# High and low parts of the row maxima by two reductions, in a two-layer cross-attention kernel

## The chip, the core and the metric

The kernel runs on one core of a Trainium2 chip. A core has five engines with instruction streams of their own that meet through semaphores: PE (TensorE: matmuls, with the weight loads listed apart as PEld), DVE (VectorE: element-wise work and reductions along the free dimension), ACT (ScalarE: activations and copies), POOL (GpSimd: element-wise work between SBUF tiles here) and SP (SyncE, which issues nearly all DMAs). Data lies in SBUF, in 128 partitions; matmuls write PSUM, which has eight banks of 128 x 512 fp32. The metric is the device time of one execution in microseconds, as a median of runs.

## The reference

Two layers over x of 4 x 512 x 320, each of them self attention, cross attention to a context of 4 x 1601 x 192, and a gated feed-forward part. There are 20 heads of 16 channels. Of one layer, cut to what matters:

```python
h1 = _ln(x, n1_g, n1_b)
x = _attn(h1, h1, q1, k1, v1, o1_w, o1_b, heads) + x
h2 = _ln(x, n2_g, n2_b)
x = _attn(h2, context, q2, k2, v2, o2_w, o2_b, heads) + x
h3 = _ln(x, n3_g, n3_b)
a, g = jnp.split(h3 @ ff_w1 + ff_b1, 2, axis=-1)
x = a * jax.nn.gelu(g, approximate=False) @ ff_w2 + ff_b2 + x
```

where `_attn` has, for each head, `sim = q k^T * scale`, `a = softmax(sim)` and `out = a v`. The softmax needs each query's maximum over the keys, or something close to it, to be taken off before the exponential; any value near it serves, since it cancels in the quotient.

## The kernel before

**Units.** Attention is cut into 80 units: layer (2) x kind (self, cross) x batch element (4) x group of four heads (5). A feed-forward unit for each layer and batch element follows the attention of its layer. Self attention has 512 keys, or 4 chunks of 128; cross attention 1601, or 13 chunks, the last with 65 rows.

**High and low parts.** Matmuls take fp32 operands in a rounded form, F32R. Queries and keys are split into a rounded high part and a low part that holds what the rounding left, and products of both are added up. POOL does this splitting (lines 803 and 804).

**A unit's two passes over the scores.** In the first pass scores stand with queries on the partitions: PE writes 128 x 512 of them into a bank (`sps`, L1054), and DVE reduces the bank to 128 maxima (L1069). In self units a maximum goes straight into the tile `nmax`, 16 columns for 4 heads x 4 blocks of 128 queries. In cross units the maxima of four stretches of keys go to `pm`, with a shorter one for the rest (L1091), and `max_reduce` (L1109) brings them together into `nmax`. In the second pass scores stand with keys on the partitions (`st`, L1280): two products of keys and queries, and a third of a tile of ones with `nrows`, which takes the maximum of each query off. ACT raises the bank (L1290), and a chunk later PE multiplies the result with the values (`av`, L1306); ACT copies that (L1325), and POOL adds it up (L1326).

**From columns to rows.** `max_end` lies between the passes. A maximum stands in a query's partition and must come to stand in a row, queries along the free dimension, and in two parts, since `nrows` is read as F32R. In `max_end`, L1119 writes the rounded maxima into a tile `parts` (the conversion), L1120 takes them from the maxima and writes the difference beside them (the subtraction), L1123 turns `parts` in blocks of 32 x 32 into `turned`, and four DMAs on SP carry rows of it into `nrows` (L1131). The minus sign comes in earlier: L1069 of a self unit and L1109 of a cross unit write the maxima negated.

**Order.** Everything is issued in one written order. While a unit's second pass runs over its chunks, the first pass of the next one or two units is mixed in, pair by pair of heads (`round_of` sets the matmuls of both in turns). Three chunks from a unit's end, `main` calls `max_reduce` and `max_end` for the next unit, whose first-pass products have all been issued by then; after that come the last two chunks, with first-pass products of the unit after next. Beside the chunks a list of errands is worked off: projections, layer norms, output projections, and POOL's divisions by the softmax's sums (L1191). Banks of PSUM are given out when the program is made, by estimated times of PE, ACT and DVE (`expect`, `busy`, `written`); a matmul into a bank waits until the last reader of it is done.

`nmax` and `nrows` exist twice and are used in turn; `parts` and `turned` come from a pool with two buffers.

Of the kernel before, what the change touches and what calls it, by code (L numbers as in the profile page):

```python
# [9 lines left out]
F32 = mybir.dt.float32  # L10
F32R = mybir.dt.float32r
I32 = mybir.dt.int32
AF = mybir.ActivationFunctionType
ALU = mybir.AluOpType
AX = mybir.AxisListType
# [8 lines left out]
P = 128  # L24
NQ = N // P
G, HG = 5, 4
GD = HG * DH
SLOT = 32
# [47 lines left out]
def kernel(ctx: ExitStack, tc: tile.TileContext, x, context, ws, out):  # L76
# [18 lines left out]
    nc = tc.nc  # L95
    dma = nc.sync.dma_start

    const = ctx.enter_context(tc.tile_pool(name="const", bufs=1))
    wpool = ctx.enter_context(tc.tile_pool(name="weights", bufs=1))
    one = ctx.enter_context(tc.tile_pool(name="one", bufs=1))  # L100
    two = ctx.enter_context(tc.tile_pool(name="two", bufs=2))
# [19 lines left out]
    nc.gpsimd.memset(columns_of, 1.0)  # L121
    vals = columns_of[:, : NC2 * H * VW].rearrange("p (c h w) -> p c h w", h=H, w=VW)

    nmax = [const.tile([P, HG * NQ], F32, name=f"nmax{i}") for i in range(2)]
    nrows = [const.tile([P, N], F32R, name=f"nrows{i}") for i in range(2)]
    for t in nrows:
        nc.gpsimd.memset(t.bitcast(F32), 0.0)
# [271 lines left out]
    def bank(name):  # L399
        i = min(range(NB), key=lambda i: bank_free[i])  # L400
        assert bank_free[i] < HELD, name
        t = psum.tile([P, 512], F32, tag=f"bank{i}", name=name)
        bank_of[id(t)] = [i, t, bank_free[i], 0.0]
        bank_free[i] = HELD
        return t
# [6 lines left out]
    def busy(engine, us, *tiles):  # L412
        expect[engine] = max([expect[engine]] + [bank_of[id(t)][3] + 0.05 for t in tiles]) + us
        for t in tiles:
            bank_free[bank_of[id(t)][0]] = expect[engine] + 0.09
# [624 lines left out]
    def max_pairs(u):  # L1040

        full = u.nkeys // 512
        rest = u.nkeys - full * 512
        ns = full + (1 if rest else 0)
        u.nm = nmax[u.n % 2]
        u.rows = nrows[u.n % 2]
        u.pm = two.tile([P, NQ, HG, ns], F32, tag="pm", name="pm") if ns > 1 else None

        def full_two(heads, t, s):
            pss = []  # L1050

            def product(e):
                for j, ps in zip(heads, pss):
                    nc.tensor.matmul(  # L1054
                        ps,
                        lhsT=u.q[j * SLOT : (j + 1) * SLOT, e, t * P : (t + 1) * P],
                        rhs=u.kT[j * SLOT : (j + 1) * SLOT, u.k0 + s * 512 : u.k0 + (s + 1) * 512],
                        start=(e == 0),
                        stop=(e == 1),
                    )  # L1060

            if ns == 1:
                to = u.nm.rearrange("p (j t) -> p j t", t=NQ)[:, :, t]
            else:
                to = u.pm[:, t, :, s]

            def reduce():
                for j, ps in zip(heads, pss):
                    nc.vector.tensor_reduce(to[:, j : j + 1], ps, AX.X, ALU.max, negate=(ns == 1))  # L1069
                    busy("dve", 0.6, ps)  # L1070

            return heads, [lambda e=e: product(e) for e in range(2)], reduce, pss, lambda: pss.extend(bank("sps") for _ in heads)

        def rest_two(heads):
            pss = []
            w = rest + rest % 2

            def product(t):
                for e in range(2):
                    for j, ps in zip(heads, pss):  # L1080
                        nc.tensor.matmul(  # L1081
                            ps[:, t * w : (t + 1) * w],
                            lhsT=u.q[j * SLOT : (j + 1) * SLOT, e, t * P : (t + 1) * P],
                            rhs=u.kT[j * SLOT : (j + 1) * SLOT, full * 512 : full * 512 + w],
                            start=(e == 0),
                            stop=(e == 1),
                        )

            def reduce():
                for j, ps in zip(heads, pss):  # L1090
                    nc.vector.tensor_reduce(  # L1091
                        u.pm[:, :, j, full], ps[:, : NQ * w].rearrange("p (t w) -> p t w", w=w)[:, :, :rest], AX.X, ALU.max,
                    )
                    busy("dve", 0.38, ps)

            return heads, [lambda t=t: (product(t), product(t + 1)) for t in range(0, NQ, 2)], reduce, pss, lambda: pss.extend(bank("sps") for _ in heads)

        pairs = [
            deque([lambda heads=heads, t=t, s=s: full_two(heads, t, s)] for s in range(full) for t in range(NQ))
            for heads in ((2, 3), (0, 1))  # L1100
        ]
        if rest:
            for q, heads in zip(pairs, ((2, 3), (0, 1))):
                q.append([lambda heads=heads: rest_two(heads)])
        return pairs

    def max_reduce(u):
        if u.pm is not None:
            nc.vector.tensor_reduce(  # L1109
                u.nm.rearrange("p (j t) -> p t j", t=NQ), u.pm, AX.X, ALU.max, negate=True  # L1110
            )
            busy("dve", 0.25)

    def max_end(u):

        parts = two.tile([P, SLOT], F32, tag="parts", name="parts")
        high, low = (parts.rearrange("p (j e t) -> p e j t", e=2, t=NQ)[:, e] for e in range(2))
        of = u.nm.rearrange("p (j t) -> p j t", t=NQ)
        nc.vector.tensor_copy(high.bitcast(F32R), of)  # L1119
        nc.vector.tensor_tensor(low, of, high, ALU.subtract)  # L1120
        turned = two.tile([P, SLOT], F32, tag="turned", name="turned")

        nc.vector.transpose(turned, parts)  # L1123
        busy("dve", 0.6)
        slots = u.rows.bitcast(F32).rearrange("(g s) n -> s g n", s=DH)[0].rearrange("g (t r) -> g t r", t=NQ)

        def rows():
            for i in range(P // SLOT):
                part = slice(i * SLOT, (i + 1) * SLOT)
                queue = (nc.sync, nc.scalar, nc.gpsimd, nc.sync)[i] if start["on"] else nc.sync  # L1130
                queue.dma_start(out=slots[:, :, part], in_=turned[part, :])  # L1131

        if u.cross and u.before.cross:
            errands.appendleft((clock["round"] + 1, yes, rows))
        else:
            rows()
# [133 lines left out]
    def main(u, give, nxt):  # L1270
# [59 lines left out]
        for c in range(u.nch):  # L1330
# [29 lines left out]
            if not last and c == u.nch - 3:  # L1360
                max_reduce(nxt)
                max_end(nxt)
# [52 lines left out]
    def ff_main(u, give, nxt):  # L1415
        done = 0

        def beside(room, n):

            nonlocal done  # L1420
            if room:
                for extra in give(done, True)[1]:
                    round_of(extra)
            done += n
            if done == u.steps - 1 and nxt is not None and nxt.kind != "ff":
                max_reduce(nxt)
                max_end(nxt)
            steps(True)
            for _ in range(n - 1):
                steps(False)  # L1430
# [235 lines left out]
    at_once(units[2])  # L1666
    run("values")
    max_reduce(first)
    max_end(first)
    loads.extend(load_x(2))  # L1670
    for fs in (load_out(0, "o1_w"), load_x(3), load_cross(0)):
# [57 lines left out]
```

## Time and profile before

| | |
|---|---|
| median of 3 runs | 3000.01 us (2998.21 to 3005.65) |
| profiled execution, its own time | 3000.91 us |
| its span, first to last instruction | 2999.1 us |
| granted TensorE clock, mean | 0.993 |
| self attention, layer 0 and layer 1 | about 60 to 375 and 1525 to 1867 us of the span |
| cross attention, layer 0 and layer 1 | about 375 to 1200 and 1867 to 2690 us |
| feed-forward, layer 0 and layer 1 | about 1200 to 1525 and 2690 to 2999 us |

How to read the profile's lines: a group has the kernel's line, the engine, the operation, the tiles written and read (out<-in), shapes as partitions x elements, and the count; behind the bar stand the busy time in us, the mean duration of one in ns, and the engine's idle time ahead of these instructions with what ended it. A row of the view of one line has minimum, median and maximum duration in ns. A row of the timeline has the start and the length in us, counted from the start of the span, and in brackets the idle time ahead of it and who ended it; instructions of one group that follow each other are merged (x8). A row of windows has the stretch, its length, and an engine's busy time with the count. Where an instruction is held up after its engine has taken it, the profile books the delay as part of its duration.

### The profile page before, as it was taken

The page shows a single profiled execution, that of the slowest core. Times are in us where ns is not written, and L with a number is a line of the kernel's source. Part 1 is how long each engine was busy: PE and PEld are TensorE (multiplying, and loading weights), DVE is VectorE, ACT ScalarE, POOL GpSimd, SP SyncE. Part 2 cuts the span into 40 slices and gives each one's busy share as a digit, 9 for nine tenths or more (in the row PEclk, how much of TensorE's full clock was granted, in tenths as well). Part 3 has the DMA queues.
Part 4 walks back from the last instruction along what each step waited for, and adds up shares of the span by engine and source line. Part 5 has one row for each costly group of instructions (what it writes and reads, how often), then busy time and mean ns, then how long its engine had stood idle before and what let it go on. Part 6 is the DMA issues. An engine that isn't in the chain of part 4 may idle for free.

```text
span 2999.1 us, 84363 instructions
## 1 busy us (share of the span) xinstructions
PE 2885.4 (96%) x35018; PEld 1509.7 (50%) x35018; DVE 2150.8 (72%) x4143; ACT 1892.7 (63%) x3746; POOL 1194.0 (40%) x1305
## 2 busy tenths in 40 slices
PE   8999999999999999999999899999999999999999
PEld 4455554555554554355554555555555555544555
DVE  6877888889889888323268788888888888873221
ACT  3766677877877878501147676778778778784000
POOL 3444344544544545211224443445445454451110
PEclk9999999999999999999999999999999999999999
DMA  4444223132232122200123342222221121222000
GB/s 107 103 122 102 71 74 96 46 90 60 53 82 67 39 56 60 82 17 15 37 60 74 91 99 66 66 58 53 53 64 46 49 70 44 54 54 76 22 22 14
DMA packets 186543, 188.70 MB, mean 63 GB/s; under 512 B 69668, under 2 KB 137264, under 8 KB 186160
## 3 DMA queue, kind: packets, MB, share of 16 engines
q1 hardware_dynamic: 185368, 182.11, 24.0%
q8 instruction: 276, 4.52, 0.6%
q10 hardware_dynamic: 760, 1.18, 0.2%
q14 instruction: 107, 0.88, 0.1%
q0 software_dynamic: 32, 0.00, 0.0%
HBM read 55.76 MB, written 29.36 MB: 28 GB/s over the span
## 4 chain that ended last, share of the span: by engine, by line
PE 77%; DVE 18%; DMA 1%; issue 1%; ACT 1%; POOL 1%; SPq 1%; ACTq 0%; DVEq 0%; POOLq 0%
PE av L1306 21%; PE st L1280 15%; PE fps L1391 9%; DVE pm L1069 9%; PE sps L1054 6%; PE yps L1498 6%; PE vps L1015 4%; DVE nmax L1069 4%; PE ops L1209 3%; PE kps L951 3%; PE qkps L886 3%; PE fps L1451 2%; PE qps L927 2%; PE sps L1081 1%; DVE hturned L608 1%
## 5 line engine op out<-in xcount | busy, mean ns | idle before, releaser
L1290 ACT ACTIVATE pr<-st 128x512 f32<-128x512 f32 (+1 forms) x2720 | 1405.0, 603 | 429.1 <-PE st L1280 381.4
L1069 DVE TENSOR_REDUCE pm<-sps 128x1 f32<-128x512 f32 x1920 | 1185.3, 681 | 129.6 <-PE sps L1054 121.5
L1326 POOL TENSOR_TENSOR o<-o,vo 128x512 f32<-128x512 f32 x576 | 740.7, 1286 | 1125.9 <-ACT vo L1325 1114.3
L1054 PE MATMUL sps<-kT,q 32*128 32x512 f32 x4800 | 874.4, 429 | 13.7 <-DMA q<-low 4.3
L1306 PE MATMUL av<-pr,vals 128*32 128x512 f32 (+1 forms) x5440 | 738.4, 609 | 74.7 <-DVE nmax L1069 19.3
L1280 PE MATMUL st<-q,kT 32*128 32x512 f32 (+1 forms) x5120 | 795.7, 421 | 7.1 <-DVE pm L1069 6.4
L1280 PEld LDWEIGHTS st<-q,kT 32*128 32x128 f32 (+1 forms) x5120 | 422.9, 180 | 299.5 <-issue 120.1
L1280 PE MATMUL st<-nrows,ones 32*128 32x512 f32 (+1 forms) x2720 | 542.6, 399 | 5.4 <-DMA nrows<-turned 5.4
L1054 PEld LDWEIGHTS sps<-kT,q 32*128 32x128 f32 x4800 | 424.0, 183 | 102.2 <-DVE pm L1069 26.8
L1069 DVE TENSOR_REDUCE nmax<-sps 128x1 f32<-128x512 f32 x640 | 395.2, 680 | 81.1 <-PE sps L1054 77.9
L1325 ACT COPY vo<-av 128x512 f32<-128x512 f32 x576 | 352.3, 612 | 26.8 <-PE av L1306 24.7
L1462 ACT ACTIVATE gl<-fps,b 128x512 f32<-128x512 f32 x80 | 54.8, 687 | 414.3 <-PE fps L1451 303.0
L1306 PEld LDWEIGHTS av<-pr,vals 128*32 128x32 f32 (+1 forms) x5440 | 111.1, 108 | 348.8 <-DVE pm L1069 180.7
L1391 PE MATMUL fps<-hT,w 128*128 128x512 f32 x640 | 283.2, 597 | 0.0
L1280 PEld LDWEIGHTS st<-nrows,ones 32*128 32x128 f32 (+1 forms) x2720 | 247.0, 180 | 28.2 <-DMA nrows<-turned 4.8
L1463 DVE SCALAR_TENSOR_TENSOR hid<-fps,b,gl 128x512 f32<-128x512 f32 x80 | 59.7, 748 | 238.8 <-ACT gl L1462 236.7
L1391 PEld LDWEIGHTS fps<-hT,w 128*128 128x128 f32 x640 | 119.2, 190 | 155.1 <-issue 152.6
L1498 PE MATMUL yps<-w,hid 128*128 128x320 f32 x640 | 176.0, 435 | 0.1
L1498 PEld LDWEIGHTS yps<-w,hid 128*128 128x128 f32 x640 | 120.4, 190 | 56.4 <-ACT gl L1462 5.3
L1209 PEld LDWEIGHTS ops<-wo,aT 112*32 112x32 f32 (+1 forms) x3072 | 98.0, 110 | 64.6 <-issue 42.9
L1209 PE MATMUL ops<-wo,aT 112*32 112x160 f32 (+1 forms) x3072 | 126.2, 301 | 0.9 <-DVE pm L1069 0.9
L1505 DVE TENSOR_TENSOR x<-yps,x 128x320 f32<-128x320 f32 x32 | 15.7, 492 | 145.9 <-PE yps L1498 145.9
(89 smaller groups left out, 2476.1 us busy)
## 6 DMA issues: line engine op xcount, KB each, us to landing
kT<-stages SPq DMA_DIRECT2D x160, 200.2 KB
oway<-o SPq DMA_DIRECT2D x80, 256.0 KB
q<-high SPq DMA_DIRECT2D x160, 64.0 KB
q<-low SPq DMA_DIRECT2D x160, 64.0 KB
kT<-high SPq DMA_DIRECT2D x60, 128.0 KB
q<-high SPq DMA_DIRECT2D x60, 128.0 KB
kT<-low SPq DMA_DIRECT2D x57, 128.0 KB
aT<-oway SPq DMA_DIRECT2D x32, 224.0 KB
```

Of the source, the lines that this page charges most:

```text
L886: nc.tensor.matmul(ps[f : f + m, :w], lhsT=wqk[:n, k, f // GD, column : column + m], rhs=first.hT[:n, k, at : at + w], start=(k == 0), sto ...
L1015: nc.tensor.matmul(ps[f : f + m, :w], lhsT=u.kvT[:n, k, at + f : at + f + m], rhs=wv[:n, k, h0 * DH : h1 * DH], start=(k == 0), stop=(k == ...
L1054: nc.tensor.matmul(ps, lhsT=u.q[j * SLOT : (j + 1) * SLOT, e, t * P : (t + 1) * P], rhs=u.kT[j * SLOT : (j + 1) * SLOT, u.k0 + s * 512 : u ...
L1069: nc.vector.tensor_reduce(to[:, j : j + 1], ps, AX.X, ALU.max, negate=(ns == 1))
L1209: nc.tensor.matmul(ps[f : f + m, : D // 2], lhsT=aT[:n, k, f * NQ + t * SLOT : f * NQ + t * SLOT + m], rhs=wo[:n, k, cols], start=(k == 0) ...
L1280: nc.tensor.matmul(own[0][:r, :], lhsT=ones[rows, :r] if e == 2 else u.keys(rows, c), rhs=u.rows[rows, :] if e == 2 else u.q[rows, e, :], ...
L1290: nc.scalar.activation(p[:r], own[0][:r], AF.Exp)
L1306: nc.tensor.matmul(ps[j * SLOT : (j + 1) * SLOT, :], lhsT=columns_of[:r, head : head + SLOT], rhs=pr.pop((c, j))[:r, :], start=True, stop= ...
L1325: nc.scalar.copy(vo, ps)
L1326: nc.gpsimd.tensor_tensor(u.o, u.o, vo, ALU.add)
L1391: nc.tensor.matmul(ps, lhsT=w1[:, k, i * FF + c * P : i * FF + (c + 1) * P], rhs=natural(u.hT[:, k]), start=start, stop=stop,)
L1498: nc.tensor.matmul(ps[:, :D], lhsT=hid[c][:, t * P : (t + 1) * P], rhs=w2[:, c, :], start=(c == 0), stop=(c == NHC - 1),)
```

## The change

The tile `nmax` becomes three times as wide: for each head it now holds the maxima (slot 0), the high part (slot 1) and the low part (slot 2), 4 columns each. The maxima are stored as they are, without the minus sign. The high part is a maximum over one element, negated and written in rounded form; the low part is a sum over two elements, maximum and high part, negated, which is the same difference as before with the sign put in here. The transpose reads slots 1 and 2 of the four heads in place, four runs of 8 columns, where it read 32 in a row; the tile `parts` is gone. The order of the instructions on each engine, their number, and the semaphores that they wait for are those of before.

```diff
-    nmax = [const.tile([P, HG * NQ], F32, name=f"nmax{i}") for i in range(2)]
+    nmax = [const.tile([P, HG, 3, NQ], F32, name=f"nmax{i}") for i in range(2)]
...
-                to = u.nm.rearrange("p (j t) -> p j t", t=NQ)[:, :, t]
+                to = u.nm[:, :, 0, t]
...
-                    nc.vector.tensor_reduce(to[:, j : j + 1], ps, AX.X, ALU.max, negate=(ns == 1))
+                    nc.vector.tensor_reduce(to[:, j : j + 1], ps, AX.X, ALU.max)
...
     def max_reduce(u):
         if u.pm is not None:
             nc.vector.tensor_reduce(
-                u.nm.rearrange("p (j t) -> p t j", t=NQ), u.pm, AX.X, ALU.max, negate=True
+                u.nm[:, :, 0, :].rearrange("p j t -> p t j"), u.pm, AX.X, ALU.max,
             )
...
     def max_end(u):
 
-        parts = two.tile([P, SLOT], F32, tag="parts", name="parts")
-        high, low = (parts.rearrange("p (j e t) -> p e j t", e=2, t=NQ)[:, e] for e in range(2))
-        of = u.nm.rearrange("p (j t) -> p j t", t=NQ)
-        nc.vector.tensor_copy(high.bitcast(F32R), of)
-        nc.vector.tensor_tensor(low, of, high, ALU.subtract)
+        top, high, low = (u.nm[:, :, i, :] for i in range(3))
+        nc.vector.tensor_reduce(
+            high.bitcast(F32R), top.rearrange("p j (t o) -> p j t o", o=1), AX.X, ALU.max, negate=True
+        )
+        nc.vector.tensor_reduce(
+            low, u.nm[:, :, 0:2, :].rearrange("p j e t -> p j t e"), AX.X, ALU.add, negate=True
+        )
         turned = two.tile([P, SLOT], F32, tag="turned", name="turned")
 
-        nc.vector.transpose(turned, parts)
+        nc.vector.transpose(turned.rearrange("p (j c) -> p j c", j=HG), u.nm[:, :, 1:3, :].rearrange("p j e t -> p j (e t)"))
```

## The prediction, made before the changed kernel ran

> **What bounds the kernel now.** I read the page first: its busy line and the chain of waits that ended last.
>
> ```profile
> span 2999.1 us, 84363 instructions
> ...
> PE 2885.4 (96%) x35018; PEld 1509.7 (50%) x35018; DVE 2150.8 (72%) x4143; ACT 1892.7 (63%) x3746; POOL 1194.0 (40%) x1305
> ...
> PE 77%; DVE 18%; DMA 1%; issue 1%; ACT 1%; POOL 1%; SPq 1%; ACTq 0%; DVEq 0%; POOLq 0%
> ```
>
> PE sets the end, but 18% of the chain lies on VectorE (DVE), so DVE time is not free. Shares are averages, so I next took busy time by stage. These two rows are the cross attention of the two layers, 1648 us of the span:
>
> ```profile
> core 0: us, PE busy (x) PEld busy (x) DVE busy (x) ACT busy (x) POOL busy (x), PEclk, DMA share, GB/s
> ...
> 375.00:1200.00 825.00, 795.27 (x11300) 419.51 (x11295) 712.08 (x1343) 646.15 (x1291) 400.50 (x390) 1.00 0.26 66
> ...
> 1867.00:2690.00 823.00, 794.73 (x11330) 419.43 (x11328) 702.85 (x1308) 648.10 (x1295) 401.33 (x390) 1.00 0.22 55
> ```
>
> There PE is busy 795 of 825 us and DVE 712, or 86%: a DVE that loses a microsecond has little room to make it up. Who waits for whom says how that reaches PE:
>
> ```profile
> PEld av L1306 <- DVE pm L1069: 180.7, 354, 1.6
> ```
>
> The weight load of the value matmuls waits 354 times for a maximum (L1069), because the eight PSUM banks come free only as DVE has reduced what stands in them. So DVE and PE turn in a ring, and what makes DVE late can make PE late.
>
> **The two instructions that go.** Now the groups of DVE instructions, with count, busy time and mean, and the same two lines by minimum, median and maximum; the reduction of the cross units' partial maxima (L1109) stands with them.
>
> ```profile
> L1069 DVE TENSOR_REDUCE pm<-sps 128x1 f32<-128x512 f32 x1920 | 1185.3, 681 | 129.6 <-PE sps L1054 121.5 <-PE st L1280 3.5
> L1091 DVE TENSOR_REDUCE pm<-sps 128x4 f32<-128x260 f32 x160 | 61.2, 425 | 31.1 <-PE sps L1081 27.8 <-PE sps L1054 0.6
> L1119 DVE CAST parts<-nmax 128x16 fp32r<-128x16 f32 x80 | 40.9, 511 | 1.5
> L1120 DVE TENSOR_TENSOR parts<-nmax,parts 128x16 f32<-128x16 f32 x80 | 23.3, 291 | 2.7
> ```
>
> ```profile
> L1119 DVE CAST parts<-nmax x80: 141/240/1297, 39.2 to 2689.5; 128x16 fp32r<-128x16 f32 x80
> ...
> L1120 DVE TENSOR_TENSOR parts<-nmax,parts x80: 174/176/1275, 39.4 to 2689.7; 128x16 f32<-128x16 f32 x80
> ...
> L1109 DVE TENSOR_REDUCE nmax<-pm x40: 206/211/223, 375.0 to 2689.2; 128x16 f32<-128x64 f32 x40
> ```
>
> Sixteen elements cannot need 1.3 us: the spread from 141 to 1297 ns is waiting that the profile books as work. For what it waits, one unit shows, first DVE, then GpSimd (POOL), then PE:
>
> ```profile
> 2344.65 0.21 DVE L1109 TENSOR_REDUCE nmax<-pm 128x16 f32<-128x64 f32 x1
> 2344.89 0.98 DVE L1119 CAST parts<-nmax 128x16 fp32r<-128x16 f32 x1
> 2345.91 1.21 DVE L1120 TENSOR_TENSOR parts<-nmax,parts 128x16 f32<-128x16 f32 x1
> ...
> 2347.29 4.83 DVE L1069 TENSOR_REDUCE pm<-sps 128x1 f32<-128x512 f32 x8
> ```
> ```profile
> 2344.56 1.29 POOL L1326 TENSOR_TENSOR o<-o,vo 128x512 f32<-128x512 f32 x1 [1.74 <-ACT vo L1325]
> 2345.80 2.51 POOL L1191 TENSOR_TENSOR aT<-aT,rT 112x512 f32<-112x512 f32 x2
> ```
> ```profile
> 2345.82 1.07 PE L1306 MATMUL av<-pr,vals 128*32 128x512 f32 x8 [0.21 <-ACT pr L1290]
> 2347.99 0.44 PE L1280 MATMUL st<-q,kT 32*65 32x512 f32 x2 [1.10 <-DVE pm L1069]
> ```
>
> The conversion ends at 2345.87, as POOL's addition ends (2345.85). The subtraction starts while POOL has gone on to the first of two multiplications of some 1.25 us, and ends with it (2347.12). The reduction L1109 ran at 2344.65 under that same addition and took its usual 0.21. So a conversion and a two-input subtraction stand behind a running POOL instruction, and a reduction does not; its maximum of 223 ns over 40 calls says the same. PE stood 1.10 us, until the first late maximum freed a bank.
>
> **The sum on DVE.** Removed: 40.9 + 23.3 = 64.2 us. Added: 80 reductions of 16 elements to 16 and 80 of 32 to 16, neither in the trace. From above, the nearest row bounds them: 211 ns with 64 elements and the same 16 results, SBUF to SBUF. From below, the conversion's fastest, 141. Between, L1069 and L1091 differ by 681 - 425 = 256 ns for 252 elements, about 1.02 ns each; off 211 that leaves 211 - 49 = 162 and 211 - 33 = 178 ns. I take these, since L1109 is the same instruction in the same memory: 80 x 0.340 = 27.2 us. DVE gets 37.0 us back (30.4 if both took 211, 41.6 if both took 141).
>
> The Trainium skill (VectorE: DVE Perf Modes, sections Rules for kernel authors and The TRN2 errata) speaks against the trade: it calls the reduction the slowest DVE operation and advises restructuring it off a hot path. By the page's measured fixed term of about 150 cycles at 0.96 GHz and one element a cycle, the pair would take 173 + 190 = 363 ns, an estimate, and the sum at the end of this part would come to 2981 where the rows give 2980. The row of 211 ns for 64 elements is already below the 223 which that arithmetic gives it, so the trace holds here.
>
> **What else the edit touches.** The maxima are no longer negated on writing (L1069, L1109), which leaves operation and shape alone. They lie with a stride of 12 in a wider tile, and the transpose reads four runs of 8 instead of one of 32; counts, the order on every engine and the semaphores waited for stay as they were. No DMA is added or moved. I put these at nothing: a one-element result has no stride to follow, and for the transpose some tens of ns are covered where DVE waits for PE behind it. Without that cover, and were the broken run to double the pace of 1.02 ns for its 32 elements, it would cost 80 x 0.033 = 2.6 us, an estimate.
>
> **How much of it lies on the path.** The two lines alone, by cross stage, L1119 first, then L1120:
>
> ```profile
> 375.00:1200.00 825.00, 15.13 (x19) 1.00 0.26 66
> 1867.00:2690.00 823.00, 14.64 (x20) 1.00 0.22 55
> ```
> ```profile
> 375.00:1200.00 825.00, 6.44 (x19) 1.00 0.26 66
> 1867.00:2690.00 823.00, 6.68 (x20) 1.00 0.22 55
> ```
>
> The 39 calls there cost 42.9 us; new, 39 x 0.340 = 13.3. So 29.6 of the 37 us come from cross attention and 7.4 from the other 41 calls. Two cross units of one layer, at the same place of successive batch elements, make a natural experiment: a stalled conversion in the first, a free one in the second, and the same score matmul some 18 us on.
>
> ```profile
> 2047.07 0.21 DVE L1109 TENSOR_REDUCE nmax<-pm 128x16 f32<-128x64 f32 x1
> 2047.31 0.83 DVE L1119 CAST parts<-nmax 128x16 fp32r<-128x16 f32 x1
> ...
> 2262.99 0.21 DVE L1109 TENSOR_REDUCE nmax<-pm 128x16 f32<-128x64 f32 x1
> 2263.23 0.18 DVE L1119 CAST parts<-nmax 128x16 fp32r<-128x16 f32 x1
> ```
> ```profile
> 2065.89 0.50 PE L1280 MATMUL st<-q,kT 32*128 32x512 f32 x2
> ...
> 2281.15 0.49 PE L1280 MATMUL st<-q,kT 32*128 32x512 f32 x2
> ```
>
> From the reduction to that matmul it is 18.82 us with the stall and 18.16 without: 0.66 us for 0.65 of stall, all of it kept. The other end is a unit in which PE was late anyway:
>
> ```profile
> 988.68 0.83 DVE L1119 CAST parts<-nmax 128x16 fp32r<-128x16 f32 x1
> ...
> 990.72 1.29 DVE L1069 TENSOR_REDUCE pm<-sps 128x1 f32<-128x512 f32 x2 [0.75 <-PE sps L1054]
> ```
>
> After the stall DVE still waits 0.75 us for PE, so nothing was lost. In the doubly stalled unit shown before, 0.98 + 1.21 - 0.34 = 1.85 us of stall made 1.10 us of idle PE, or 0.6, before any backlog. Shares of 1, 0 and at least 0.6; I take 0.65 for cross: 19.2 us. Self attention has more room, as a stalled unit and the free one after it show:
>
> ```profile
> 133.27 0.93 DVE L1119 CAST parts<-nmax 128x16 fp32r<-128x16 f32 x1
> ...
> 134.70 2.48 DVE L1069 TENSOR_REDUCE nmax<-sps 128x1 f32<-128x512 f32 x4
> ...
> 147.22 0.16 DVE L1119 CAST parts<-nmax 128x16 fp32r<-128x16 f32 x1
> ...
> 148.64 2.48 DVE L1069 TENSOR_REDUCE nmax<-sps 128x1 f32<-128x512 f32 x4 [0.81 <-PE sps L1054]
> ```
>
> From the conversion to the next maximum it is 1.43 us with the stall and 1.42 without: the free one spends the difference waiting for PE. Not every self unit has such a pause, so I take a little. Share 0.2: 1.5 us. Sum 20.7 us, against the profiled execution's 3000.9 us (span 2999.1 and 1.8 around it): 2980.2. That execution lies 0.9 above the median of 3000.0, well within 2998.2 to 3005.7, so I forecast 2980. What is late next is PE's own pace and its waits for ScalarE's exponentials.
>
> **The rivals.**
> Everything counts (chance 0.10): the ring passes every stall on, as in the twin units, self attention included: 3000.9 - 37.0 = 2964. Against it: the unit at 988.68.
> Hidden anyway (0.11): most units are like 988.68, with a share under 0.25; PE's 96% speaks for it, the 1.10 us idle against it. Share 0.15: 5.6 us, 2995.
> It does not do what it says (0.04): the reductions wait for POOL too, through their new layout or their rounded output. L1109 under the running addition speaks against it. Time 3001.
> Slower, by re-phasing (0.05): other DVE instructions stand behind POOL as well, above all the normalisation, whose fastest and slowest are far apart:
>
> ```profile
> L562 DVE TENSOR_SCALAR hn<-x,mv,root x64: 423/446/1503, 494.4 to 2895.3; 128x320 f32<-128x320 f32 x64
> ```
>
> With DVE earlier, more of these 64 may start under a POOL instruction. From the median to the maximum is 1.06 us each, 68 us at most, 44 on the path at 0.65, net +23: 3024. It decides only if the typical one loses over 20.7 / 0.65 / 64 = 0.5 us, and is slower by 9 us from 0.71 us on. Some already pay, and POOL's own work is no longer than before, which is against it.
>
> **How the numbers follow.** The forecast has 0.70, with a range of its own from 2970 to 2990 (shares 0.8 and 0.3 of 37 us). The range reaches down to the full 37 us, 2964, and up to 7.9 us of gain, 2993; the 0.20 of the last three rivals lie outside. A difference of 0.3%, 9 us, is about what a measurement of this kernel can tell from none. Faster than that are the forecast and the full saving, 0.80; within it the hidden case and the one that does nothing, 0.15; slower 0.05.
>
> **What would show it.** In the changed kernel's profile the two new reductions should keep a minimum and maximum within some 30 ns of each other, near 162 and 178 ns, also while POOL runs; DVE busy should fall from 2150.8 to about 2114; the transpose should stay at 0.21; and the cross windows should shrink by some 10 us each, the idle PE ahead of the short last chunk (the 65-row matmul at 2347.99) with them. The mechanism is wrong if the reductions reach a microsecond; the share is wrong if DVE loses its 37 us and the span keeps its length. New stalls on L562 would show the slower rival.

## The result

The changed kernel takes 2982.86 us (median of 6 runs) against 3001.51 of before (median of 6), a ratio of 0.9935 with a 95% interval of 0.9921 to 0.9949: 18.6 us faster, where 20 were forecast. One of the six runs took 5353 us and is left out of the ratio; without it the median would be 2982.20 us. The page of the changed kernel's profiled execution (2982.2 us, span 2980.4) answers to the lines quoted for before:

```profile
span 2980.4 us, 84363 instructions
...
PE 2874.4 (96%) x35018; PEld 1511.5 (51%) x35018; DVE 2119.6 (71%) x4143; ACT 1889.8 (63%) x3746; POOL 1193.4 (40%) x1305
...
PE 79%; DVE 16%; ACT 1%; DMA 1%; issue 1%; POOL 1%; SPq 0%; ACTq 0%; POOLq 0%; DVEq 0%
```

DVE is busy 31.2 us less, and its share of the chain fell from 18% to 16%. The view of the tile `nmax` has the two new reductions and the transpose, by minimum, median and maximum in ns:

```profile
L1117 DVE TENSOR_REDUCE nmax<-nmax x80: 135/169/172, 39.9 to 2670.7; 128x16 fp32r<-128x16 f32 x80
L1120 DVE TENSOR_REDUCE nmax<-nmax x80: 185/187/192, 40.1 to 2670.9; 128x16 f32<-128x32 f32 x80
L1125 DVE STREAM_TRANSPOSE turned<-nmax x80: 211/211/216, 40.3 to 2671.2; 128x32 f32<-128x32 f32 x80
```

The longest of 160 calls took 192 ns, where the conversion and the subtraction had reached 1297 and 1275. The transpose's four short runs cost nothing. The unit that had stalled twice in before, at 2344.65, stands in the changed kernel's timeline so, first DVE, then POOL, then PE:

```profile
2332.06 0.21 DVE L1109 TENSOR_REDUCE nmax<-pm 128x16 f32<-128x64 f32 x1
2332.30 0.17 DVE L1117 TENSOR_REDUCE nmax<-nmax 128x16 fp32r<-128x16 f32 x1
2332.51 0.19 DVE L1120 TENSOR_REDUCE nmax<-nmax 128x16 f32<-128x32 f32 x1
2332.73 0.21 DVE L1125 STREAM_TRANSPOSE turned<-nmax 128x32 f32<-128x32 f32 x1
2332.87 3.64 DVE L1069 TENSOR_REDUCE pm<-sps 128x1 f32<-128x512 f32 x6
```
```profile
2331.97 1.29 POOL L1328 TENSOR_TENSOR o<-o,vo 128x512 f32<-128x512 f32 x1 [1.73 <-ACT vo L1327]
2333.22 2.54 POOL L1193 TENSOR_TENSOR aT<-aT,rT 112x512 f32<-112x512 f32 x2
```
```profile
2333.23 1.06 PE L1308 MATMUL av<-pr,vals 128*32 128x512 f32 x8 [0.21 <-ACT pr L1292]
...
2334.23 0.45 PE L1282 MATMUL st<-q,kT 32*65 32x512 f32 x2
```

POOL runs the same three instructions at the same place, and all of DVE's work passes under the first of them. PE goes from the value matmuls to the next scores in 1.00 us without a pause, where it took 2.17 with 1.10 of them idle. How long the cross stages take is read from the first and the last start of the cross units' reduction, L1109, in each layer; before and after:

```profile
L1109 DVE TENSOR_REDUCE nmax<-pm x20: 206/211/223, 375.0 to 1201.3; 128x16 f32<-128x64 f32 x20
L1109 DVE TENSOR_REDUCE nmax<-pm x20: 206/211/221, 1867.3 to 2689.2; 128x16 f32<-128x64 f32 x20
```
```profile
L1109 DVE TENSOR_REDUCE nmax<-pm x20: 206/211/222, 377.7 to 1193.1; 128x16 f32<-128x64 f32 x20
L1109 DVE TENSOR_REDUCE nmax<-pm x20: 206/211/222, 1859.3 to 2670.5; 128x16 f32<-128x64 f32 x20
```

That is 826.3 and 821.9 us before, 815.4 and 811.2 after: 10.9 + 10.7 = 21.6 us, more than the whole gain. The first start also shows what was given back, 375.0 against 377.7. Up to there the two kernels differ only by the edit in the self units, and in the five kernels below that are the changed kernel up to there, this start lies between 375.5 and 377.3; so loading and self attention vary by some 2 us from one trace to another, and this pair stands unfavourably there.

### The profile page after: what moved, and what is told of

It is laid out like the page before. It is cut to its first block, busy times and chain, and to the rows that moved or that the text cites. A ratio compares the mean times of both kernels' runs of the same rounds, so it can differ in the third digit from the quotient of the medians.

```text
span 2980.4 us, 84363 instructions
## 1 busy us (share of the span) xinstructions
PE 2874.4 (96%) x35018; PEld 1511.5 (51%) x35018; DVE 2119.6 (71%) x4143; ACT 1889.8 (63%) x3746; POOL 1193.4 (40%) x1305
## 4 chain that ended last, share of the span: by engine, by line
PE 79%; DVE 16%; ACT 1%; DMA 1%; issue 1%; POOL 1%; SPq 0%; ACTq 0%; POOLq 0%; DVEq 0%
PE av L1308 22%; PE st L1282 16%; PE fps L1393 9%; DVE pm L1069 8%; PE sps L1054 6%; PE yps L1500 6%; PE vps L1015 5%; DVE nmax L1069 4%; PE kps L951 4%; PE ops L1211 3%; PE qkps L886 3%; PE fps L1453 2%; PE qps L927 2%; PE sps L1081 1%; ACT pr L1292 1%; DVE hturned L608 1%
## 5 line engine op out<-in xcount | busy, mean ns | idle before, releaser
L1069 DVE TENSOR_REDUCE pm<-sps 128x1 f32<-128x512 f32 x1920 | 1187.2, 682 | 136.3 <-PE sps L1054 125.8
L1069 DVE TENSOR_REDUCE nmax<-sps 128x1 f32<-128x512 f32 x640 | 395.7, 681 | 85.9 <-PE sps L1054 83.0
L886 PE MATMUL qkps<-hT,wqk 96*32 96x256 f32 (+1 forms) x1920 | 121.3, 395 | 0.0
```

The source lines that it names most:

```text
L886: nc.tensor.matmul(ps[f : f + m, :w], lhsT=wqk[:n, k, f // GD, column : column + m], rhs=first.hT[:n, k, at : at + w], start=(k == 0), sto ...
L1069: nc.vector.tensor_reduce(to[:, j : j + 1], ps, AX.X, ALU.max)
```

## The experiments

The theory: the conversion and the subtraction stand behind whatever POOL is executing, a reduction does not, and the time that DVE loses there is passed on to PE. Rivals: the new layout makes the gain; rounding or dependence made the waits; DVE's time is hidden and the gain came otherwise. In the table, "cross" is the sum of the two lengths just shown, "set back" the time from the start of L1109 to the start of the transpose, summed over the 40 cross units, less that of the changed kernel (26.9 us); both are worked out from the traces.

| kernel | median us | ratio to before, interval | cross us | set back us |
|---|---|---|---|---|
| before | 3001.51 | | 1648.2 | 28.9 |
| changed | 2982.86 | 0.9935 [0.9921, 0.9949] | 1626.6 | 0 |
| high part alone by reduction | 2989.21 | 0.9961 [0.9949, 0.9973] | 1633.2 | 17.2 |
| low part alone by reduction | 2996.55 | 0.9982 [0.9974, 0.9991] | 1640.8 | 23.2 |
| layout alone | 3002.36 | 0.9998 [0.9988, 1.0009] | 1648.8 | 29.0 |
| one idle reduction more | 2995.33 | 0.9979 [0.9970, 0.9987] | 1638.5 | 22.5 |
| two idle reductions more | 3012.10 | 1.0037 [1.0024, 1.0049] | 1659.7 | 49.6 |
| idle copy of 16 | 2996.25 | 0.9983 [0.9974, 0.9992] | 1642.5 | 23.2 |
| idle reduction of 16 | 2980.60 | 0.9931 [0.9918, 0.9943] | 1630.6 | 0.3 |
| no low part | 2975.06 | 0.9911 [0.9898, 0.9925] | 1623.6 | -17.1 |
| before without POOL's additions | 2975.41 | 0.9908 [0.9893, 0.9923] | 1622.3 | -0.3 |
| changed without POOL's additions | 2975.65 | 0.9908 [0.9891, 0.9924] | 1622.2 | -0.1 |

**The high part alone.** Before, with the conversion replaced:

```diff
-        nc.vector.tensor_copy(high.bitcast(F32R), of)
+        nc.vector.tensor_reduce(high.bitcast(F32R), of.rearrange("p j (t o) -> p j t o", o=1), AX.X, ALU.max)
```

> Before with one line changed: the high part comes from a reduction over one element, the low part still from the subtraction. Theory (a two-input subtraction stands behind a running POOL instruction as the conversion did): the subtraction now starts while POOL is still at the same addition and takes over most of the waiting, so its mean rises from 291 to about 550 ns or more while the new reduction stays near 165; of the 36 us of DVE time that the whole change saved, at most 10 come back, and the time is 2995 to 3002 us. Rival (each instruction has a wait of its own, and the two add up): the conversion's own 27 us of waiting are gone, the subtraction's mean stays at 291 ns, and three quarters of the 18.6 us gain come, 2986 to 2989 us.

It took 2989.21 us, between what the theory and the rival gave. The view of the tile `parts`:

```profile
L1119 DVE TENSOR_REDUCE parts<-nmax x80: 136/169/172, 40.9 to 2678.9; 128x16 fp32r<-128x16 f32 x80
L1122 DVE TENSOR_TENSOR parts<-nmax,parts x80: 174/178/1286, 41.1 to 2679.1; 128x16 f32<-128x16 f32 x80
```

and the doubly stalled unit in its timeline:

```profile
2338.69 0.21 DVE L1109 TENSOR_REDUCE nmax<-pm 128x16 f32<-128x64 f32 x1
2338.94 0.17 DVE L1119 TENSOR_REDUCE parts<-nmax 128x16 fp32r<-128x16 f32 x1
2339.15 0.78 DVE L1122 TENSOR_TENSOR parts<-nmax,parts 128x16 f32<-128x16 f32 x1
2339.96 0.21 DVE L1125 STREAM_TRANSPOSE turned<-parts 128x32 f32<-128x32 f32 x1
```

The subtraction does take the conversion's place behind POOL: its mean rose from 291 to 458 ns. But it comes 0.21 us later and waits that much less, and where two POOL instructions follow each other there is now one wait of 0.78 us, not 0.98 and 1.21, since the subtraction gets in as the first ends (POOL's addition ends at 2339.90, the subtraction at 2339.93). The waits neither add up nor move over whole; I had sized the move too large.

**The low part alone.** The changed kernel, with the high part by an instruction with one input again:

```diff
-        nc.vector.tensor_reduce(high.bitcast(F32R), top.rearrange("p j (t o) -> p j t o", o=1), AX.X, ALU.max, negate=True)
+        nc.vector.tensor_scalar(high.bitcast(F32R), top, -1.0, None, ALU.mult)
```

> The changed kernel with the high part made by one-input instruction again (the maxima times -1, written in rounded form); the low part comes from the reduction. Theory: the first instruction waits for POOL as the conversion did, mean near 500 ns, and where a second POOL instruction followed the reduction does not wait for it, at 187 ns; some 9 of 36 us of DVE time are saved, time 2994 to 2999 us. Rival (the gain belongs to the layout or to the reduction of the low part): 2983 to 2987 us.

```profile
L1117 DVE TENSOR_SCALAR nmax<-nmax x80: 142/227/1298, 39.7 to 2686.4; 128x16 fp32r<-128x16 f32 x80
L1118 DVE TENSOR_REDUCE nmax<-nmax x80: 186/188/191, 39.9 to 2686.6; 128x16 f32<-128x32 f32 x80
```

2996.55 us, as the theory had it: a multiplication by a constant waits just as the conversion did, and the reduction behind it does not. Both halves of the edit are needed; alone they give 12 and 5 us.

**The layout alone.** The wide tile and the transpose in place, with the conversion and the subtraction writing into it, and the maxima negated on writing:

```diff
-        nc.vector.tensor_reduce(high.bitcast(F32R), top.rearrange("p j (t o) -> p j t o", o=1), AX.X, ALU.max, negate=True)
-        nc.vector.tensor_reduce(low, u.nm[:, :, 0:2, :].rearrange("p j e t -> p j t e"), AX.X, ALU.add, negate=True)
+        nc.vector.tensor_copy(high.bitcast(F32R), top)
+        nc.vector.tensor_tensor(low, top, high, ALU.subtract)
```

> The changed kernel's wide tile, without parts and with the transpose reading slots in place, but with the maxima negated on writing and the conversion and subtraction of before. Theory: the waits behind POOL are all there again, means near 511 and 291 ns, and the time is that of before, 2998 to 3005 us; the transpose stays at 211 ns. Rival (the layout makes the gain): 2981 to 2986 us.

The two instructions by line, with count, busy us and mean ns:

```profile
L1117 DVE CAST nmax<-nmax 128x16 fp32r<-128x16 f32 x80 | 40.9, 512 | 1.5
L1118 DVE TENSOR_TENSOR nmax<-nmax 128x16 f32<-128x16 f32 x80 | 23.3, 291 | 2.8
```

Means of 512 and 291 ns, a ratio of 0.9998: the layout changes nothing, and that rival falls.

**A delay that has nothing to do with POOL.** The changed kernel with a reduction that nobody reads:

```diff
         top, high, low = (u.nm[:, :, i, :] for i in range(3))
+        if u.cross:
+            nc.vector.tensor_reduce(
+                spent[:, :5], ident[:, :120].rearrange("p (o n) -> p o n", o=1).to_broadcast([P, 5, 120]), AX.X, ALU.max
+            )
```

> The changed kernel with one more reduction of 600 elements, whose result nobody reads, ahead of the high part in the cross units only: a fixed delay of DVE, 40 times about 0.75 us or 30 us, at the place where the conversion waited, and nothing that meets POOL. Theory (what the waits cost was DVE's lateness at that place, passed on at the 0.74 which the two traces show for cross units): 2983 + 22, 3001 to 3009 us. Rival (DVE's time there is mostly hidden, and the gain came by another way, as by POOL being held up less): 2983 to 2990 us.

2995.33 us met neither. One unit in its timeline, DVE alone:

```profile
2298.84 0.21 DVE L1110 TENSOR_REDUCE nmax<-pm 128x16 f32<-128x64 f32 x1
2298.96 0.77 DVE L1119 TENSOR_REDUCE spent<-ident 128x5 f32<-128x600 f32 x1
2299.65 0.16 DVE L1122 TENSOR_REDUCE nmax<-nmax 128x16 fp32r<-128x16 f32 x1
```

An instruction of 0.77 us set DVE back by only 0.56: it depends on nothing, so it starts 0.09 us before its predecessor's end, and the next one, whose input is long there, 0.08 before its own. So the delay was smaller than I had put it, 22.5 us in all. And its cost per unit was not one share. By the group g of the unit whose maxima are split, the medians over the units that were set back at all:

| g | before: set back, cost us | one reduction more | two more | slack |
|---|---|---|---|---|
| 0 | 0.39, 0.35 | 0.56, 0.52 | 1.24, 1.20 | 0.04 |
| 1 | 1.83, 0.97 | 0.56, 0.01 | 1.24, 0.38 | 0.86 |
| 2 | 0.89, 0.35 | 0.55, 0.08 | 1.24, 0.75 | 0.5 |
| 3 | 0.79, 0.46 | 0.56, 0.27 | 1.24, 0.95 | 0.3 |
| 4 | 0.65, 0.65 | 0.56, 0.53 | 1.24, 1.23 | 0.0 |

(Cost is the time from one unit's L1109 to the next one's, less the same in the changed kernel.) Every unit passes on its lateness less a slack of its own, the part that lengthens nothing, whatever made it late. The group is not all that sets it: the prediction's unit at 988.68 has g = 4, as the twins have, and passed on nothing of 0.65 us in before, of 0.56 with one reduction more, or of 1.24 with two. It takes 44.3 us to the next L1109 in all these kernels, where the other five of its group take 41.1 in the changed one.

**Twice the delay** was to tell this from a fixed share; the edit is the same with two such reductions, which write different elements.

> The changed kernel with two of the 600-element reductions that nobody reads in the cross units, where one of them had set DVE back by 0.56 us and cost 12.5 us in all. The second should set it back by about 0.70 more, 1.26 us in each unit. Theory (each unit passes on its lateness less a slack of its own, by its place g among the five groups: about 0.05, 0.85, 0.54, 0.28 and 0 us for g = 0 to 4): 33 us over the changed kernel, 3012 to 3019 us. Rival (one share for all units, 0.55 as with a single delay): 28 us, 3008 to 3011.5 us. Second rival (0.74, as between the two kernels): 37 us or more, over 3019 us.

```profile
L1110 DVE TENSOR_REDUCE nmax<-pm x20: 206/211/221, 376.9 to 1209.4; 128x16 f32<-128x64 f32 x20
L1110 DVE TENSOR_REDUCE nmax<-pm x20: 206/210/221, 1872.7 to 2699.9; 128x16 f32<-128x64 f32 x20
```

The cross stages took 832.5 + 827.2 = 1659.7 us, 33.1 over the changed kernel's, as the slacks had it; the median rose by 29.2, at the low edge of the range and only 0.6 above that of the fixed share, so it is the cross stages that tell the two apart. The table's third pair of numbers has the same slacks within 0.05 us. A fixed 0.55 would have given 28 us in the cross stages.

**A copy and a reduction of 16 elements** at the same place, read by nobody and rounding nothing:

```diff
+        if u.cross:
+            nc.vector.tensor_copy(spent, ident[:, :16])
```
```diff
+        if u.cross:
+            nc.vector.tensor_reduce(spent, ident[:, :16].rearrange("p (t o) -> p t o", o=1), AX.X, ALU.max)
```

> The changed kernel with a copy of 16 fp32 elements that nobody reads, ahead of the high part in the cross units: no rounding, no dependence, only a one-input SBUF copy at the place where POOL's addition runs. Theory (an instruction of that kind stands behind a running POOL instruction): minimum near 0.15 us, mean over 0.5, maximum near 1.3, and a time like that of the run that had only the first instruction put back, 2992 to 3000 us. Rival (the waits came from the rounding to F32R, or from waiting for the maxima): mean under 0.2 us, 2983 to 2986 us.

> The same with a reduction over one element each of the same 16 elements in place of the copy. Theory: minimum and maximum within 40 ns, about 0.17 us, start to start less than 0.1 us since nothing depends on it; 2982 to 2985 us. Rival (any further instruction at that place costs the same): as the run with the copy.

The view of the tile `spent`, of the copy and then of the reduction:

```profile
L1119 DVE COPY spent<-ident x40: 161/950/1197, 376.3 to 2683.9; 128x16 f32<-128x16 f32 x40
```
```profile
L1119 DVE TENSOR_REDUCE spent<-ident x40: 154/158/161, 375.6 to 2671.0; 128x16 f32<-128x16 f32 x40
```

Copying sixteen elements a partition takes 0.95 us in the median, reducing the same sixteen 0.158. The copy costs 13 us, the reduction nothing (2980.60, a little under what I had given): it fits into the gap in which L1120 waits for L1110's result. So neither rounding nor dependence makes the wait, but the kind of instruction. The Trainium skill (SBUF — State Buffer, section Who interferes with whom) gives a cause for it: VectorE and GpSimd share a pair of SBUF ports, held for a whole instruction; copies, casts and operations with a constant can take it, an operation with two SBUF inputs takes its reading half, a reduction on trn2 never does. The rows agree on which of them wait: copy, conversion, multiplication by a constant and subtraction have maxima of 1197, 1297, 1298 and 1275 ns, the reductions of 16 elements 161 and 172. That it is a port that is held, no run here shows.

**POOL taken away.** If POOL's instruction is what they wait for, the old pair must be as fast without it. In before and in the changed kernel, POOL's additions of three chunks are left out, so that those chunks' products are missing in the output of the cross units:

```diff
-                nc.gpsimd.tensor_tensor(u.o, u.o, vo, ALU.add)
+                if not u.cross or c not in (8, 9, 10):
+                    nc.gpsimd.tensor_tensor(u.o, u.o, vo, ALU.add)
```

> Before, with POOL's addition of the ninth to eleventh chunk's values left out in cross units (those products are missing in the output): POOL is then idle where the next unit's maxima are split, but for the divisions (L1191) in one unit of five. Theory (the conversion and the subtraction wait for POOL's running instruction and for nothing else): in cross units both stay near 0.17 to 0.25 us except beside L1191, their mean there falls from 0.76 and 0.34 us to under 0.35 and 0.30, and the time is at most 8 us over the next run's, 2980 to 2992 us. Rival (they wait for something else that happens at that place, such as a queue or another engine's access): the durations stay, 2997 us or more.

> The changed kernel with the same additions left out (those products are missing in the output). Theory: POOL's additions bound nothing, so the time is the changed kernel's, 2978 to 2985 us, and the gap to the run before falls from 18.6 us to between 0 and 8 us. Rival (POOL's work as such is on the path): it gains 5 us or more over the changed kernel.

Before without the additions, the conversion in the cross units of each layer:

```profile
L1119 DVE CAST parts<-nmax x20: 174/175/177, 375.9 to 1188.3; 128x16 fp32r<-128x16 f32 x20
```
```profile
L1119 DVE CAST parts<-nmax x20: 174/175/176, 1854.5 to 2664.3; 128x16 fp32r<-128x16 f32 x20
```

All 40 conversions take 174 to 177 ns, and the gap between the two kernels is gone: 2975.41 and 2975.65 us. That settles who is waited for. What I had not expected is that the changed kernel itself gains 7 us without the additions, which the rival had said, so both times lie under the theory's ranges; 4.4 us of it lie in the cross stages. The traces show through what. These rows are of the unit at 2332.06 shown above, SP and PE in the changed kernel, and then of the same unit without the additions, DVE, SP and PE:

```profile
2334.53 0.54 SPq L1186 DMA_DIRECT2D rT<-rway  x1
2335.18 2.69 SPq L1133 DMA_DIRECT2D nrows<-turned  x4
2339.06 0.49 PE L1282 MATMUL st<-nrows,ones 32*128 32x512 f32 x2 [0.62 <-DMA nrows<-turned]
```
```profile
2328.20 0.21 DVE L1109 TENSOR_REDUCE nmax<-pm 128x16 f32<-128x64 f32 x1
2329.14 2.69 SPq L1133 DMA_DIRECT2D nrows<-turned  x4
2334.39 0.39 PE L1282 MATMUL st<-nrows,ones 32*128 32x512 f32 x1
```

With the additions the four DMAs into `nrows` are issued 3.12 us after L1109, without them 0.94, and PE's wait of 0.62 us for them is gone. They stand on SP behind the load of `rT` for a later division (L1186), which starts 0.03 us after POOL's first division ends, and that division runs behind the addition. So it is in six of the eight units with g = 1, in before as in the changed kernel; without the additions these six are 0.8 to 1.7 us shorter, 6.1 in all, and one other unit is 1.7 us longer. The usual 0.8 to 0.9 is also the slack of g = 1, 0.86: DVE may be that late where `nrows` is late anyway. That match is no proof, as no run moved the load alone.

**A version without the low part.** The softmax is shifted by the rounded maximum alone, the same for every key, so it cancels in the quotient:

```diff
-                    nc.vector.tensor_reduce(to[:, j : j + 1], ps, AX.X, ALU.max)
+                    nc.vector.tensor_reduce(to[:, j : j + 1], ps, AX.X, ALU.max, negate=(ns == 1))
...
-                u.nm[:, :, 0, :].rearrange("p j t -> p t j"), u.pm, AX.X, ALU.max,
+                u.nm[:, :, 0, :].rearrange("p j t -> p t j").bitcast(F32R), u.pm, AX.X, ALU.max, negate=True
...
-        top, high, low = (u.nm[:, :, i, :] for i in range(3))
...
-        nc.vector.transpose(turned.rearrange("p (j c) -> p j c", j=HG), u.nm[:, :, 1:3, :].rearrange("p j e t -> p j (e t)"))
+        nc.vector.transpose(turned.rearrange("p (j c) -> p j c", j=HG), u.nm.rearrange("p j e t -> p j (e t)"))
```

> The low part is left out: the softmax is shifted by the rounded maximum alone, which cancels in the quotient; the maxima are negated and rounded where they are reduced (L1069, L1109), both instructions behind them are gone, and slot 1 holds zeros. DVE is 0.43 us earlier in every unit than in the changed kernel. Theory (slack by place): only the units without slack, g = 4, can gain, 7 of them up to 0.4 us, and self units little: 2978 to 2983 us. Rival (a share of 0.74 in cross units for earliness as for lateness): 13 us, 2969 to 2972 us.

```profile
L1111 DVE TENSOR_REDUCE nmax<-pm x20: 207/210/223, 375.2 to 1188.4; 128x16 fp32r<-128x64 f32 x20
L1111 DVE TENSOR_REDUCE nmax<-pm x20: 206/210/221, 1853.0 to 2663.4; 128x16 fp32r<-128x64 f32 x20
```

It beats both kernels, 2975.06 us, a ratio of 0.9911 to before; that is 3 us under the theory's range and 3 over the rival's. The cross stages gained 1626.6 - 1623.6 = 3.0 us from 17.1 us of earliness, so they hardly pass on DVE's being early, as the theory had it; by the medians only g = 4 gains, some 0.1 us a unit. The other 5 us came from outside them, partly from a start that was quicker in this trace than in the changed kernel's (375.2 against 377.7). How much of that is the self units' two instructions less was not separated.

## Why the prediction was right

**What bounds the kernel, and the mechanism.** Right. The waits were booked as durations, they ended with POOL's instructions, and they were passed on to PE through the banks. The copy, the reduction of 16 elements and the two kernels without POOL's additions show it; the prediction had it from L1109 alone. One row of the prediction does not carry this, though: the value matmuls' weight load, 180.7 us of waiting there, waits as long in the changed kernel. What fell are above all the waits of the score matmuls of both passes, as the prediction's other row, PE's 1.10 us ahead of `st`, had it; weight loads in before, and then after:

```profile
PEld st L1280 <- DVE pm L1069: 49.1, 112, 2.0
PEld sps L1054 <- DVE pm L1069: 27.7, 82, 1.0
```
```profile
PEld av L1308 <- DVE pm L1069: 179.4, 354, 1.6
PEld st L1282 <- DVE pm L1069: 38.0, 96, 0.8
PEld sps L1054 <- DVE pm L1069: 15.8, 46, 1.0
```

So a long wait for DVE in the profile is not by itself time that a faster DVE gives back.

**The sum on DVE.** By line, with busy us and mean ns, the changed kernel has

```profile
L1120 DVE TENSOR_REDUCE nmax<-nmax 128x16 f32<-128x32 f32 x80 | 15.0, 187 | 2.8
L1117 DVE TENSOR_REDUCE nmax<-nmax 128x16 fp32r<-128x16 f32 x80 | 13.1, 164 | 1.5
```

28.1 us where 27.2 were worked out (162 and 178 ns from L1109 and a slope), so 36.1 came off the two lines, not 37.0. DVE's whole busy time fell by 31.2 only: it is a union, and some other groups grew, L1069 by 2.4 us. The forecast of 2114 left that out.

**What else the edit touches.** Nothing, as said; the layout alone measured 0.9998.

**The share on the path.** This is the term that was mis-sized, in both halves, and the errors met. For cross I took 0.65 of 29.6, 19.2 us; 21.6 were measured, against 28.9 of set back, 0.75. But 0.75 is no property of the kernel. The shares of 1, 0 and 0.6 that the prediction read off three units were three different slacks (none, over 1.24 us, and 0.86), and averaging them came near by luck: the medians of the table, times the units that were set back, give some 18 us, and most of the rest lies in three units of 38 whose intervals were 1.5 to 1.8 us longer in before than that, one of them without being late at all. Two such jumps of 1.6 to 1.7 us also stand in the trace with the idle reduction of 16, in units whose DVE was not set back; so a few us of any one trace come from something that the lateness does not explain. For self attention I took 0.2 of 7.4, 1.5 us; there was nothing to see: in layer 1 the transposes of the first self unit and the first cross unit lie 0.3 us further apart in the changed kernel, and the part up to the first cross unit took 2.7 longer.

**The rivals.** The full 37 us did not come, since three of five groups have slack. Hidden anyway is true of g = 1 up to 0.86 us and of the unit at 988.68, but before had set g = 1 back by 1.83. The re-phasing rival would have shown in the normalisation's line, which after reads

```profile
L562 DVE TENSOR_SCALAR hn<-x,mv,root x64: 426/446/1507, 496.7 to 2876.6; 128x320 f32<-128x320 f32 x64
```

with the minimum, median and maximum of before within 4 ns: it waits for POOL as it did, and no more.

## What to carry to other kernels

Look at minimum and maximum of a short DVE instruction, not at its mean: 141 and 1297 ns for sixteen elements is a wait in disguise, and what ends when the long ones end is what it waits for. A small copy, cast or subtraction between SBUF tiles beside a busy POOL can be had as a reduction, which does not wait here; replace all of a chain's waiting instructions, or the next one inherits part of the wait. What a delay costs is its length less the slack of the place, so a share measured at one delay does not hold at another, and earliness beyond the slack is worth little. And look at when a DMA is issued as well as at when its input is ready: it can stand in its queue behind one that waits for another engine.

## What was not expected of the hardware

Two DVE instructions of which the second depends on nothing overlap: with 0.21 us from 2298.84, the next began at 2298.96, and a reduction of 0.77 us cost 0.56, one of 0.158 us nothing at all. The Trainium skill (VectorE: DVE Perf Modes, section The DRAIN you can't avoid) has the next operation start only when the pipeline is empty, and adds that one which is not held starts earlier. The trace agrees with the addition: here the independent one starts 0.08 to 0.09 us before its predecessor's recorded end, while a dependent one starts some 0.03 us after it (2332.06 + 0.21, then 2332.30).
